# A four-layer decoder: state space decays as two 64x64 products, and new times in the planner's table

## The chip, the cores and the metric

One core of one Trainium2 chip runs the whole program. The metric is device time in microseconds (us) for one execution. A core has five engines that work side by side, each on its own queue of instructions in a fixed order: TensorE (PE in the profile: matrix products; PEld is its loading of weights), VectorE (DVE), ScalarE (ACT), GpSimd (POOL) and SyncE (SP, which issues transfers). An engine that reaches an instruction whose input isn't there waits, and everything queued behind it waits too.

## The reference

The input is 2048 tokens (32 sequences of 64) of 256 values. Twelve sublayers follow each other, each added to its input:

```python
x = x + _L0_attn_ref(_layernorm(x, axis=-1), ...)
x = x + _L0_xattn_ref(_layernorm(x, axis=-1), ctx_1024, ...)
x = x + _L0_ffn_ref(...)
x = x + _L1_attn_ref(...)    # state space model, 32 heads of 64, state 128
...
x = x + _L2_attn_ref(...)    # state space model, 8 heads of 64, state 128
...
x = x + _L3_ffn_ref(...)     # 64 experts, 6 of them for each token
return x
```

The change touches the two state space layers. Their core is a scan over the 64 steps of a sequence:

```python
dt = jax.nn.softplus(dt + dt_bias)
A = -jnp.exp(A_log)
dA = jnp.exp(dt * A)
def step(h, inp):
    dA_t, dt_t, x_t, B_t, C_t = inp
    u = (dt_t[:, :, None] * x_t)[..., None] * B_t[:, :, None, :]
    h = dA_t[:, :, None, None] * h + u
    y = jnp.einsum('bhpn,bhn->bhp', h, C_t)
    return (h, y)
```

A sequence is only 64 steps long, so the scan can be written as a 64x64 matrix for each head: entry (s, t) is C_t . B_s times the decay from s to t, which is the exponential of the sum of dt*A over the steps after s up to t.

## The kernel before

**Two layers of code.** The kernel doesn't call the engines in order. A Recorder (`net.nc`) takes each operation with its operands and finds what it depends on. When all of them are recorded, the class Order goes through them with a list schedule: it keeps a time for each engine (`free_at`), looks at the operations whose inputs will be there, and always takes the one that can start earliest, the recorded order breaking ties. Its result fixes the order of the instructions on all five engines, the buffers that tiles get, and the engine of each operation that may run on one of two (`either`: VectorE or ScalarE; `combine`: VectorE or GpSimd). The function issue then emits the program in this order; its line 2326 is therefore the line of every instruction in the profile.

**What the planner believes.** `duration` (line 456) gives each operation a time from its engine, its kind and the number of its elements; `latency` (line 488) is what passes between the end of an operation and the start of one on another engine that needs it. In `Order.run` an engine is free again at start + cost. An operation that needs one on its own engine alone may start, for the planner, when the first has started: the order of the queue keeps them apart. Nothing of this table is on the chip. It decides the order alone; the chip waits on semaphores, so an order planned with wrong times is still a correct one. Operations up to 120 us of TensorE work ahead of the oldest unfinished one may be planned (`Order(net.nc.ops, Net.SLOTS, 120.0)`).

**What is recorded.** Tokens are worked on in 16 tiles of 128 (two sequences each), in three groups of 8, 6 and 2 tiles. While a group goes through the last sublayers, the next goes through the first ones, and the recorder weaves the two. The state space layers work on two tiles (256 tokens) at a time and on eight heads at a time: `unit_ssm_heads` (line 1229) is called 4 times for each pair of tiles in the first of these layers and once in the second, so (4 + 1) x 8 = 40 times.

**The decays.** In `unit_ssm_heads`, `ra` is dt*A of the two tiles, eight heads and 64 columns, zero where the column comes before the row. The constant `after` (line 53) is a 128x128 matrix with a one where the row comes later than the column *and both are in the same sequence*: two 64x64 triangles on the diagonal, zeros elsewhere. `after` times `ra[:, t]` adds up the steps between. For each of the two tiles t that is one product with 128 rows, 128 columns of weights and 512 moving columns into one 512-wide PSUM tile `ps`; ScalarE then takes the exponential into `m`, VectorE multiplies with C.B. Later sixteen small 64x64 products of each tile use `m`; there, the halves b = 0 and b = 1 of the partitions write PSUM tiles of their own (`pv[b]`), as in the other places where 64-row products of the two halves occur (`cross_out`: a new `po` for each b).

Of the kernel before, what the change touches and what calls it, by code (L numbers as in the profile page):

```python
# [216 lines left out]
def split(ap, a, pat="p (a b) -> p a b"):  # L217
    return ap.rearrange(pat, a=a)
# [233 lines left out]
DMA = ("dma_start", "indirect_dma_start")  # L452
# [3 lines left out]
def duration(engine, method, args, kw):  # L456

    out = kw["out"] if "out" in kw else args[0]
    if method in DMA:
        return 0.06 if engine == "sync" else 1.3  # L460
    views = [v for v in [*args, *kw.values()] if isinstance(v, View)]
    n = max(v.size() for v in views)
    if engine == "tensor":
        lhsT, rhs = args[1], args[2]
        if method == "transpose":
            return 0.109
        k, m, n = lhsT.n, lhsT.size(), rhs.size()
        part = (32 if k <= 32 else 64 if k <= 64 else 128) * (32 if m <= 32 else 64 if m <= 64 else 128) / 16384

        if part == 1:  # L470
            return max(n, m) * 0.00168 + 0.004
        return max(0.068, n * 0.00168 * part * 1.2 + 0.02)
    small = any(v.size() == 1 and v.n > 1 for v in views) and n > 1
    if engine == "vector":
        return 0.15 + n * 0.00104 + 0.06 * small
    if engine == "scalar":
        return 0.115 + n * 0.00092 + 0.08 * small
    if method == "memset":
        return 0.2 + n * 0.0004
    if ALU.pow in args:  # L480
        return 0.4 + 0.157 * n
    if method == "tensor_copy":
        return 0.25 + n * 0.001
    full = sum(all(s for s, _ in v.dims) and v.size() == n for v in views[1:])
    return 0.14 + n * (0.00174 if full < 2 else 0.0022)


def latency(engine, op):

    return 0.25 if engine == "tensor" else 0.12  # L490


RESERVE = 4
# [2 lines left out]
class Order:  # L496
# [54 lines left out]
    def elsewhere(self, o, engine, since, end):  # L551


        for w, m in o.ways:
            if w != engine:
                other = max(self.free_at[w], since) + duration(w, m, o.args, o.kw)
                gain = {"vector": 1.0, "gpsimd": -1.0}[w] if {w, engine} == {"vector", "gpsimd"} else 0.0
                if other + gain < end:
                    return True
        return False  # L560

    def run(self):
        ready = {e: [] for e in self.ENGINES}

        def enter(op):
            for e, _ in op.ways:
                bisect.insort(ready[e], op, key=lambda o: o.at)

        for o in self.ops:
            if o.waits == 0:  # L570
                enter(o)
        done, oldest, result = [False] * len(self.ops), 0, []
        while len(result) < len(self.ops):
            limit = self.pos[oldest] + self.horizon
            best = None
            for e in self.ENGINES:
                now, seen = self.free_at[e], 0
                for o in ready[e]:
                    if self.pos[o.at] > limit or seen == 32:
                        break  # L580
                    seen += 1
                    since = o.ready
                    opens = [t for t in o.tiles if t.slot is None and t.tag in self.slots]
                    if opens:
                        if any(not self.free[t.tag] for t in opens):
                            continue
                        since = max([since] + [self.free[t.tag][0][0] for t in opens])
                    start = max(now, since)
                    method = next(m for w, m in o.ways if w == e)
                    cost = duration(e, method, o.args, o.kw)  # L590
                    key = start
                    if e == "scalar":
                        table = TABLES.get(getattr(o.args[2], "name", "") if method == "activation" else "", 0)
                        if table and table != self.table:
                            key += 1.3
                            cost += 1.3
                    if len(o.ways) > 1 and self.elsewhere(o, e, since, start + cost):
                        continue
                    if best is not None and (key, o.at) >= best[0] and not (
                        o is best[1] and start + cost < best[3] + best[4]  # L600
                    ):
                        continue
                    if opens and not self.may_open(o):
                        continue
                    best = ((key, o.at), o, e, start, cost, opens)
                    if key <= now:
                        break
            assert best is not None, "nothing can go on"
            _, o, e, start, cost, opens = best
            for w, _ in o.ways:  # L610
                ready[w].remove(o)
            for t in opens:
                t.slot = self.free[t.tag].pop(0)[1]
            end = start + cost
            self.free_at[e] = end
            if e == "scalar":
                m = next(m for w, m in o.ways if w == e)
                table = TABLES.get(getattr(o.args[2], "name", "") if m == "activation" else "", 0)
                self.table = table or self.table
            lat = latency(e, o)  # L620
            if o.ways[0][1] in DMA:
                v = next(v for v in o.outs + o.ins if isinstance(v, View) and v.dtype != I32)
                self.moved = max(self.moved, end) + v.n * v.size() * 4 / 300e3
                lat = 2.0 + self.moved - end
            for t in o.tiles:
                t.left -= 1
                if t.left == 0 and t.tag in self.slots:
                    bisect.insort(self.free[t.tag], (end + lat, t.slot))
            for n in o.after:
                same = len(n.ways) == 1 and n.ways[0][0] == e and o.ways[0][1] not in DMA  # L630
                n.ready = max(n.ready, start if same else end + lat)
                n.waits -= 1
                if n.waits == 0:
                    enter(n)
            done[o.at] = True
            while oldest < len(done) and done[oldest]:
                oldest += 1
            oldest = min(oldest, len(done) - 1)
            result.append((o, e))
        self.length = max(self.free_at.values())  # L640
        return result


class Net:
# [584 lines left out]
    def unit_ssm_heads(self, W, nh, g, j, st):  # L1229

        nc = self.nc
# [7 lines left out]
        ra = self.b4(2, 8, 64)  # L1239
# [5 lines left out]
            self.conv(par, cw, xs[:, u : u + 2, :], self.pair(wx, (j + u) * P, hT), j + u)  # L1245
        gs, m = self.b4(4, GT), self.b4(2, 8, 64)
        for t in range(2):
            ps = self.mm()
            self.prod(ps, [(self.k("after"), ra[:, t])])
            nc.scalar.activation(m[:, t], split(ps, 8), AF.Exp)  # L1250
        nc.vector.tensor_tensor(m, m, bc(cb, 2, 8), ALU.mult)
        for u in range(0, 4, 2):
# [2 lines left out]
        for t in range(2):  # L1255
            ps = split(self.mm(), 4)
# [11 lines left out]
        for t in range(2):  # L1268
            for u in range(4):
                for b in range(2):  # L1270
                    rb = slice(64 * b, 64 * b + 64)
                    for h in range(2):
# [4 lines left out]
                            start=True,  # L1277
                            stop=True,
# [17 lines left out]
        for u in range(4):  # L1296
# [4 lines left out]
            for t in range(2):  # L1301
# [4 lines left out]
                    start=(first and u == 0),  # L1306
                    stop=(last and u == 3),
# [830 lines left out]
    def experts(self, n):  # L2138
# [4 lines left out]
        for i in range(n):  # L2143
            self.unit_L3_parts(i)
            yield 0.2 / n

    def unit_L3_ffn(self, layer, W, g, run):
        nc = self.nc
        gate, su, sd = W
# [5 lines left out]
        for t in range(2):  # L2155
# [21 lines left out]
            nc.vector.reduce_sum(hot, one.rearrange("p k e -> p e k"), AX.X)  # L2177
            pn = self.mm()[:, :64]
            self.prod(pn, [(self.k("before"), hot)] + ([(self.k("ones"), run)] if i else []))
            if dense:  # L2180

                nc.vector.scalar_tensor_tensor(wn[:, t], sc, wr, hot, ALU.mult, ALU.mult)
                nc.vector.scalar_tensor_tensor(wn[:, t], pn, float(P), wn[:, t], ALU.is_lt, ALU.mult)
                nc.vector.tensor_tensor(run, run, hot, ALU.add)
                continue
# [239 lines left out]
```

## Time and profile before

| | |
|---|---|
| six runs before | median 3199.26 us (3193.6 to 3208.91) |
| the profiled execution | 3205.06 us, of which 3203.3 us between its first and last instruction |
| PE busy | 2993.4 us in 26862 products |
| DVE busy | 2216.9 us in 5239 instructions |
| ACT busy | 1414.0 us in 2623 |
| POOL busy | 1414.7 us in 1278 |
| products with `after` (128x512) | 79.6 us in 160 records |
| 64x64 products on 512 columns, in cross_out | 75.2 us in 512 records |

TensorE works on these 32-bit operands in two passes, so each recorded product is two records: 80 products with `after` are 160 records. Records of PE overlap, since a product's last results come out while the next one streams in; the time that a product really takes up is the distance from its start to the next start. VectorE's records overlap too: the lengths of all its records add up to 2434 us, while it is busy for 2216.9 us; ScalarE's add up to 1537 us against 1414.0 us.

### The profile page before, as it was taken

Reading aid. Unit: us, or ns where it says so; the run is one execution under the profiler, and the core shown is the slowest. Engines: PE = TensorE matmul, PEld = TensorE weight load, DVE = VectorE, ACT = ScalarE, POOL = GpSimd, SP = SyncE. Lnnn points to the kernel's source line nnn. Section 1 sums busy time; section 2 is a strip of 40 time slices with the busy share of each in tenths; the row PEclk is TensorE's granted clock in tenths of the full one; section 3 lists DMA queues with packets and bytes.
Section 4 is the critical chain, followed back from the end, with each engine's and each line's share of the span. In section 5 each row is a group of like instructions: output and inputs, shape, how many; then the busy total and the mean of one; then the engine's idle time right before and its main releaser. Section 6 shows DMA issues by size and latency. Waiting matters only on the chain.

```text
span 3203.3 us, 66434 instructions
## 1 busy us (share of the span) xinstructions
PE 2993.4 (93%) x26862; PEld 2382.5 (74%) x26862; DVE 2216.9 (69%) x5239; ACT 1414.0 (44%) x2623; POOL 1414.7 (44%) x1278
## 2 busy tenths in 40 slices
PE   8999999999999899999989999999999988986689
PEld 7888887777777788778767777767787767774467
DVE  5564347775457577665889987777667888776684
ACT  1233226565442233534545665553335745453341
POOL 4442233224454555225653356655534655354230
PEclk9999999999999899999999999999899999997689
DMA  4104120031421433011010010203561211224240
GB/s 153 33 23 171 54 96 1 3 141 57 200 107 47 156 110 117 31 64 61 27 47 10 8 58 8 79 17 127 180 217 62 88 43 41 76 85 128 80 176 27
DMA packets 112949, 256.97 MB, mean 80 GB/s; under 512 B 26309, under 2 KB 73688, under 8 KB 100228
## 3 DMA queue, kind: packets, MB, share of 16 engines
q1 hardware_dynamic: 97860, 204.73, 18.4%
q0 software_dynamic: 14784, 48.01, 4.4%
q8 instruction: 212, 3.47, 0.5%
q14 instruction: 93, 0.76, 0.1%
HBM read 177.34 MB, written 78.77 MB: 80 GB/s over the span
## 4 chain that ended last, share of the span: by engine, by line
PE 67%; DVE 20%; ACT 5%; POOL 5%; issue 3%; DMA 1%; SPq 0%; DVEq 0%; POOLq 0%; ACTq 0%
PE L_xattn_mm L2326 9%; PE cross_out_mm L2326 8%; PE L_attn_mm L2326 8%; PE ssm_heads_mm L2326 7%; PE pair_mm L2326 5%; DVE ssm_heads_b L2326 5%; PE L_ffn_mm L2326 4%; PE turn_mm L2326 4%; PE L_block_mm L2326 3%; PE rope_mm L2326 3%; DVE L_xattn_b L2326 2%; PE L_dense_mm L2326 2%; PE heads_mm L2326 2%; PE L_experts_mm L2326 2%; PE outrows_mm L2326 1%
## 5 line engine op out<-in xcount | busy, mean ns | idle before, releaser
L2326 PE MATMUL pair_mm<-norm_b,load_ssm_w 128*128 128x256 f32 x1280 | 306.4, 385 | 0.9 <-DVE ssm_heads_b L2326 0.6
L2326 PEld LDWEIGHTS pair_mm<-norm_b,load_ssm_w 128*128 128x128 f32 x1280 | 238.4, 192 | 44.4 <-issue 8.5
L2326 DVE SCALAR_TENSOR_TENSOR ssm_heads_b<-pair_mm,load_ssm_wp,ssm_heads_b 128x252 f32<-128x252 f32 (+2 forms) x480 | 218.7, 473 | 18.4 <-ACT ssm_heads_b L2326 8.5
L2326 POOL TENSOR_TENSOR L_xattn_sm<-L_xattn_sm,__init___consts 128x8 f32<-128x8 f32 (+2 forms) x62 | 178.5, 2882 | 88.2 <-DVE L_xattn_sm L2326 79.6
L2326 ACT ACT_TABLE_LOAD x153 | 196.3, 1283 | 33.8 <-PE L_block_mm L2326 11.7
L2326 POOL TENSOR_TENSOR norm_sm<-norm_sm,__init___consts 128x1 f32<-128x1 f32 (+1 forms) x142 | 88.8, 628 | 266.1 <-DVE norm_sm L2326 252.1
L2326 ACT COPY L_xattn_b<-L_xattn_mm 128x512 f32<-128x512 f32 x189 | 110.8, 588 | 189.0 <-PE L_xattn_mm L2326 188.8
L2326 ACT COPY turn_b<-turn_mm 128x512 f32<-128x512 f32 x202 | 113.1, 588 | 182.2 <-PE turn_mm L2326 178.9
L2326 PE MATMUL ssm_heads_mm<-load_ssm_w,ssm_heads_b 128*128 128x256 f32 x640 | 161.1, 396 | 6.7 <-issue 3.7
L2326 PE MATMUL rope_mm<-norm_b,load_L_attn_w 128*128 128x128 f32 x1280 | 160.8, 282 | 3.5 <-DMA load_L_attn_w<-in_a_wk 2.9
L2326 PEld LDWEIGHTS rope_mm<-norm_b,load_L_attn_w 128*128 128x128 f32 x1280 | 152.7, 196 | 8.7 <-issue 5.7
L2326 POOL TENSOR_TENSOR ssm_heads_b<-ssm_heads_b,ssm_heads_b 128x1024 f32<-128x1024 f32 x30 | 70.8, 2362 | 188.6 <-DVE ssm_heads_b L2326 142.4
L2326 PEld LDWEIGHTS ssm_heads_mm<-load_ssm_w,ssm_heads_b 128*128 128x128 f32 x640 | 119.4, 194 | 41.9 <-issue 19.8
L2326 PEld LDWEIGHTS L_xattn_mm<-norm_b,load_L_xattn_w 128*128 128x128 f32 x1024 | 119.4, 192 | 8.3 <-issue 7.0
L2326 PE MATMUL L_xattn_mm<-norm_b,units_L_xattn_w 128*128 128x128 f32 x1024 | 122.5, 277 | 2.1 <-ACT norm_b L2326 1.4
L2326 ACT ACTIVATE ssm_heads_b<-pair_mm,load_ssm_wp 128x256 f32<-128x256 f32 x160 | 81.6, 561 | 96.8 <-PE pair_mm L2326 94.9
L2326 POOL DMA_INDIRECT slots<-norm_b,L_ffn_sm x84 | 93.4, 1112 | 68.8 <-DVE L_ffn_b L2326 24.5
L2326 PE MATMUL L_xattn_mm<-norm_b,load_L_xattn_w 128*128 128x128 f32 x1024 | 123.1, 276 | 0.0
L2326 PEld LDWEIGHTS L_xattn_mm<-norm_b,units_L_xattn_w 128*128 128x128 f32 x1024 | 118.3, 192 | 4.3 <-ACT norm_b L2326 1.8
L2326 DVE TENSOR_TENSOR rope_b<-rope_mm,__init___consts 128x512 f32<-128x512 f32 x160 | 102.7, 679 | 25.1 <-PE rope_mm L2326 13.9
L2326 PE MATMUL cross_out_mm<-load_L_xattn_w,cross_out_b 128*128 128x256 f32 x512 | 118.1, 388 | 1.9 <-ACT cross_out_b L2326 1.9
L2326 PE MATMUL L_attn_mm<-load_L_attn_w,L_attn_b 128*128 128x256 f32 x512 | 119.3, 385 | 0.7 <-ACT L_attn_b L2326 0.5
(437 smaller groups left out, 7768.1 us busy)
## 6 DMA issues: line engine op xcount, KB each, us to landing
queue<-far_w SPq DMA_DIRECT2D x14, 1024.0 KB
L_block_w<-in_f_rows SPq DMA_DIRECT2D x16, 770.0 KB
load_ssm_w<-in_s_in SPq DMA_DIRECT2D x12, 1024.0 KB
parts<-far_w SPq DMA_DIRECT2D x10, 1024.0 KB
slots<-far_w SPq DMA_DIRECT2D x16, 548.0 KB
L_experts_b<-slots SPq DMA_DIRECT2D x32, 274.0 KB
units_L_xattn_w<-kept_x SPq DMA_DIRECT2D x8, 1024.0 KB
L_parts_b<-parts SPq DMA_DIRECT2D x14, 512.0 KB
```

The source lines that it names most:

```text
L2326: done = getattr(getattr(nc, e), method)(*map(real, op.args), **{k: real(v) for k, v in op.kw.items()})
```

## The change

There are two parts. The first replaces the product with `after` by two, one for each sequence, on 64 partitions and 64 columns of weights each; both write the same PSUM tile, on different partitions. The second rewrites the planner's `duration` for VectorE, ScalarE and GpSimd, shortens `latency`, lets an engine be free again a little before the operation's result is there (`EARLY`; `got` is the time of the result), and lets an operation that needs one on its own engine start 0.03 us after that one's result instead of at its start, except on TensorE and SyncE. The times of TensorE products are left as they are; for the planner, a 128x128 product on 512 columns takes 512 x 0.00168 + 0.004 = 0.864 us, and a 64x64 one 512 x 0.00168 x 0.25 x 1.2 + 0.02 = 0.278 us.

```diff
     if method in DMA:
-        return 0.06 if engine == "sync" else 1.3
+        return 0.06 if engine == "sync" else 1.28
...
     small = any(v.size() == 1 and v.n > 1 for v in views) and n > 1
+    psum = any(v.t.psum for v in views)
+    full = sum(all(s for s, _ in v.dims) and v.size() == n for v in views[1:])
     if engine == "vector":
+        if not psum and method in ("tensor_scalar", "tensor_copy", "tensor_scalar_add", "tensor_single_scalar"):
+            return 0.16 + n * 0.00052 + 0.11 * small
+        if method == "tensor_tensor" and not full and n > 64:
+            return 0.15 + n * 0.00205
+        if method.startswith("reduce") and views[1].dims[-1][0] > 1:
+            return 0.15 + n * 0.0017
         return 0.15 + n * 0.00104 + 0.06 * small
     if engine == "scalar":
-        return 0.115 + n * 0.00092 + 0.08 * small
+        if method == "activation":
+            return (0.17 if psum else 0.205) + n * 0.00083 + 0.18 * (small and psum)
+        return 0.16 + n * 0.00084 + 0.1 * small
     if method == "memset":
-        return 0.2 + n * 0.0004
+        return 0.2 + n * 0.00066
...
+EARLY = {"vector": 0.082, "scalar": 0.1, "gpsimd": 0.04}
+
 def latency(engine, op):
 
-    return 0.25 if engine == "tensor" else 0.12
+    return 0.2 if engine == "tensor" else 0.06
...
-            end = start + cost
+            got = start + cost
+            end = got if o.ways[0][1] in DMA else got - EARLY.get(e, 0.0)
             self.free_at[e] = end
...
-                    bisect.insort(self.free[t.tag], (end + lat, t.slot))
+                    bisect.insort(self.free[t.tag], (got + lat, t.slot))
             for n in o.after:
                 same = len(n.ways) == 1 and n.ways[0][0] == e and o.ways[0][1] not in DMA
-                n.ready = max(n.ready, start if same else end + lat)
+                n.ready = max(n.ready, (start if e in ("tensor", "sync") else got + 0.03) if same else got + lat)
...
         for t in range(2):
+
             ps = self.mm()
-            self.prod(ps, [(self.k("after"), ra[:, t])])
+            for b in range(2):
+                rb = slice(64 * b, 64 * b + 64)
+                nc.tensor.matmul(ps[rb], self.k("after")[rb, rb], ra[rb, t], start=True, stop=True)
             nc.scalar.activation(m[:, t], split(ps, 8), AF.Exp)
```

More of the change, by code (lines that the diff above doesn't have):

```diff
@@ L483, in duration @@
         return 0.25 + n * 0.001
-    full = sum(all(s for s, _ in v.dims) and v.size() == n for v in views[1:])
     return 0.14 + n * (0.00174 if full < 2 else 0.0022)
+EARLY = {"vector": 0.082, "scalar": 0.1, "gpsimd": 0.04}
 def latency(engine, op):
-    return 0.25 if engine == "tensor" else 0.12
+    return 0.2 if engine == "tensor" else 0.06
 RESERVE = 4
@@ L622, in run @@
                 v = next(v for v in o.outs + o.ins if isinstance(v, View) and v.dtype != I32)
-                self.moved = max(self.moved, end) + v.n * v.size() * 4 / 300e3
-                lat = 2.0 + self.moved - end
+                self.moved = max(self.moved, got) + v.n * v.size() * 4 / 300e3
+                lat = 2.0 + self.moved - got
             for t in o.tiles:
```

## The prediction

> **What bounds the kernel now.** I read the page first: busy times, then the slices.
>
> ```profile
> span 3203.3 us, 66434 instructions
> PE 2993.4 (93%) x26862; PEld 2382.5 (74%) x26862; DVE 2216.9 (69%) x5239; ACT 1414.0 (44%) x2623; POOL 1414.7 (44%) x1278
> ...
> PE   8999999999999899999989999999999988986689
> ...
> PEclk9999999999999899999999999999899999997689
> ...
> PE 67%; DVE 20%; ACT 5%; POOL 5%; issue 3%; DMA 1%; SPq 0%; DVEq 0%; POOLq 0%; ACTq 0%
> ```
>
> TensorE sets the time: 93% busy, and 67% of the chain that ended last. It is idle for 3203.3 - 2993.4 = 210 us, and that is all that a better order can win directly. The busy times by stretch of 200 us show where this lies (the columns after the length: PE, PEld, DVE, ACT, POOL, granted clock, share of the DMA engines, GB/s).
>
> ```profile
> 400.00:600.00 200.00, 198.53 (x1465) 162.55 (x1464) 133.91 (x311) 93.84 (x151) 65.27 (x55) 1.00 0.12 39
> 1600.00:1800.00 200.00, 181.22 (x1718) 139.93 (x1716) 175.07 (x393) 109.34 (x195) 92.72 (x76) 0.97 0.07 23
> 2600.00:2800.00 200.00, 179.81 (x1844) 140.02 (x1842) 170.82 (x393) 91.81 (x197) 101.25 (x96) 0.97 0.15 49
> 2900.00:3000.00 100.00, 63.65 (x622) 44.59 (x621) 65.66 (x266) 31.54 (x67) 39.94 (x40) 0.74 0.44 135
> 3000.00:3100.00 100.00, 73.63 (x744) 51.42 (x745) 72.34 (x206) 42.56 (x85) 36.72 (x36) 0.74 0.20 72
> ```
>
> Up to 1000 us TensorE is nearly gapless. From 2900 to 3100, near the end, it idles 63 of 200 us and runs at a granted clock of 0.74; the whole end from 2800 on holds 78 us of idle time. The remaining 210 - 78 = 132 us are spread over the stretches before, the two largest pieces (19 and 20 us) where VectorE is busy for over 170 of 200 us. What TensorE waits for, by the view of waits:
>
> ```profile
> PE norm_mm L2326 <- DVE norm_b L2326: 26.3, 12, 7.9
> PE small_scores_mm L2326 <- ACT keys_apart_b L2326: 17.0, 13, 2.8
> PE turn_mm L2326 <- POOL L_xattn_b L2326: 15.1, 8, 5.4
> ```
>
> Three engines and many short waits: a matter of order, not of one late producer.
>
> **Part one, the two blocks.** The 80 products become 160, the PE records 160 become 320, with 160 more loads of weights; no DMA, no work on another engine, no new wait but that the exponential needs both halves. What does the array's time do? I read the timeline of PE (start, us, then the group):
>
> ```profile
> 581.36 1.88 PE L2326 MATMUL ssm_heads_mm<-ssm_heads_b,__init___consts 128*128 128x512 f32 x4
> 583.08 0.59 PE L2326 MATMUL pair_mm<-norm_b,load_ssm_w 128*128 128x256 f32 x2
> ...
> 278.62 1.95 PE L2326 MATMUL cross_out_mm<-turn_b,context_cx 64*64 64x512 f32 x16
> ...
> 1277.69 0.60 PE L2326 MATMUL ssm_heads_mm<-__init___consts,ssm_heads_b 128*128 128x128 f32 x4
> 1278.22 0.64 PE L2326 MATMUL L_attn_mm<-turn_b,L_attn_b 64*64 64x256 f32 x2
> 1278.79 0.44 PE L2326 MATMUL ssm_heads_mm<-__init___consts,ssm_heads_b 128*128 128x128 f32 x2
> ```
>
> Two full products (4 records) take 583.08 - 581.36 = 1.72 us, 0.43 a pass. The sixteen records of cross_out are eight 64x64 products: they start four at a time, one on each quarter of the array, every 0.43 us, and 4 x 0.43 = 1.72 us is the whole group without its end. So a quarter streams 512 columns no faster than the whole array; only using all four quarters gains. The change uses two of the four, those on the diagonal: 2 x 0.43 = 0.86 us a tile, as before. Streaming: 80 x (0.86 - 0.86) = **0**. The planner, which books 2 x 0.278 = 0.556 us, believes it saves 25 us; the rows show none of it.
>
> What is added is the change of shape. Before 1278.22, four records of 128 columns should stream 4 x 0.107 = 0.43 us, but 0.53 pass: 0.10 lost on the way in. The two records of 256 columns should take 0.43 us, but 0.57 pass: 0.14 lost. The first pass of 128x128 after such a change takes about 0.11 us longer, because its weights can't be loaded ahead. About 0.35 us for a visit. I counted the neighbours of the products with `after` in the order of PE's records: they stand in 45 groups, 32 of them between 128x128 products on both sides, 13 with a smaller shape on one side (there the change of shape only moves). 32 x 0.35 = **+11 us**, on the engine that sets the time, nothing covering it. A plan that places the visits beside other 64-row work brings it to 0; one that splits every pair makes it 80 x 0.35 = 28.
>
> No row shows one thing: two products of different partition halves writing one PSUM tile at once. Everywhere in this kernel the halves have tiles of their own. Bounds: side by side, 0.86 us a tile; one after the other, 4 passes of 0.43 = 1.72. I take the first, since neither rows of the array nor output partitions are shared; the second is a rival. The Trainium skill, TensorEngine Tiling (Array Packing), section "Gotcha 1: PSUM Pressure", speaks against the change here: different row tiles cannot access the same PSUM bank at the same time. By that rule the sum would get the 80 x 0.86 us of that rival; no run here shows it. The same page's "Theoretical Speedup" gives up to 2x for a dimension of 64, which would be a gain; the row of cross_out shows that it comes only with the other quarters filled.
>
> **Part two, the table.** It costs the chip nothing; it moves instructions. First, is it nearer to the rows?
>
> ```profile
> L2326 ACT ACTIVATE ssm_heads_b<-pair_mm,load_ssm_wp 128x256 f32<-128x256 f32 x160 | 81.6, 561 | 96.8 <-PE pair_mm L2326 94.9 <-PE L_xattn_mm L2326 1.0 <-DVE ssm_heads_b L2326 0.6
> L2326 DVE TENSOR_TENSOR ssm_heads_b<-ssm_pre,__init___consts 128x1024 f32<-128x1024 f32 x7 | 14.3, 2041 | 0.0
> L2326 POOL MEMSET values_b<- 128x576 f32 x32 | 18.6, 580 | 10.1 <-PE pair_mm L2326 7.3 <-PE small_scores_mm L2326 1.4 <-DVE L_attn_b L2326 0.8
> ```
>
> The first: 0.431 us by the old formula, 0.563 by the new, 0.561 in the trace. The second: 1.21, 2.25, 2.04. The third: 0.43, 0.58, 0.58. The application of the norm on VectorE (192 of them): 0.476 and 0.403, with a median of 0.410 and a mean of 0.535. `EARLY` follows the overlap of records: VectorE's lengths sum to 2434 us against 2217 busy, so the old table booked this engine 217 us too full, ScalarE 1537 - 1414 = 123. So the old planner took VectorE for 9% slower than it is, just where (1600 to 1800, 175 of 200 us) it is nearly full, sent work to GpSimd instead, and let products come late in TensorE's queue.
>
> What that is worth, no row prices. Upper bound of the gain: all the spread idle time, 132 us, and none is reached by a plan that still has to wait for DMA and chains; lower: a loss, worked out as a rival. The long end is a chain of dependent steps (TensorE idle there at 63 and 74 busy of 100), which an order shortens little. I take a quarter of the spread time, **-33 us**, since the errors corrected are 5 to 10% of the other engines' times and the waits are short.
>
> Sum: 3205.1 + 0 + 11 - 33 = 3183, a change of -22. The profiled execution is 5.8 us above the median of the six runs; on the median, 3199.3 - 22 = 3177. I predict **3177 us**; with the gain between 15 and 70 and the visits between 0 and 28, some 3130 to 3195.
>
> **The rivals.**
>
> *The halves write one after the other.* For it: every other place keeps them apart. Against: different output partitions. 80 x 0.86 = 69 us on TensorE: 3177 + 69 = 3246. It decides as soon as more than 22/0.86, about 26, of the 80 pairs are serialized.
>
> *The plan is too tight.* The old one had slack by mistake; the new one has none, and where VectorE and GpSimd slow each other the new times are too short: the norms' mean of 0.535 against 0.403 is 192 x 0.13 = 25 us, and the 55 subtractions and scalings of 1024 elements on VectorE at 1.3 to 1.9 us in place of 1.215 another 20. Each is a wait in a fixed queue, mostly in 1600 to 2000 and 2600 to 2800. If these 45 us come back at TensorE and the gain of 33 falls away: 3199 + 11 + 45 = 3255 at most, about half of it likely, 3232. Slower from the point where less than 11 us of idle time go.
>
> *It cancels.* The plan wins about what the visits cost: 3199 + 11 - 11 = 3199. For it: the waits are short and TensorE is 93% full anyway.
>
> **Chances.** Forecast 0.55, cancels 0.15, too tight 0.18, one after the other 0.12. About 0.3%, 10 us, is what a measurement tells from no change: below 3190 faster, above 3209 slower. A tenth of the forecast's share falls inside; a few hundredths of the cancelling case fall on either side: faster 0.54, same 0.16, slower 0.30. The range leaves out the far ends: 3120 to 3246.
>
> **What would show it.** The 320 records of 64x64 on `after`: pairs that start within 0.01 us and a next pass 0.43 us later (right), or starts 0.43 us apart for the halves (the first rival). PE busy up by about 11 us or less, idle time before 2800 us down from 132 to about 100, the GpSimd count of 1024-element operations down. Wrong would be a stretch of 200 us with more than 30 us of new idle time, or a longer end after 2800: I have assumed that the end stays.

## The result and the profile after

The changed kernel takes a median of 3221.55 us over 30 runs (3205.05 to 3265.55), the kernel before 3205.66 us over 67 runs beside it: a ratio of **1.0052, 95% interval 1.0040 to 1.0064**. It is slower by half a per cent, where 0.7% faster was forecast. The profiled execution after has a span of 3218.6 us. Its page:

```profile
span 3218.6 us, 66679 instructions
PE 3000.6 (93%) x27022; PEld 2360.8 (73%) x27022; DVE 2119.3 (66%) x5260; ACT 1418.3 (44%) x2637; POOL 1360.9 (42%) x1233
...
PE   8999999999999999999989999999999999986689
...
PEclk9999999999999999999989999999999999997689
...
PE 66%; DVE 20%; ACT 5%; POOL 4%; issue 3%; DMA 2%; SPq 0%; DVEq 0%; POOLq 0%; ACTq 0%
```

TensorE has 7 us more to do. It is idle for 3218.6 - 3000.6 = 218 us against 210. VectorE is busy for 98 us less, although the lengths of its records add up to 2434.8 us (2434.0 before): the same work, packed closer. GpSimd has 54 us less. So the new table did move and pack the work of the other engines, and the engine that sets the time got nothing of it. The stretches that the prediction read, after:

```profile
400.00:600.00 200.00, 195.95 (x1346) 154.15 (x1347) 117.84 (x289) 88.46 (x145) 68.44 (x57) 1.00 0.10 35
1600.00:1800.00 200.00, 180.95 (x1763) 136.43 (x1764) 168.69 (x414) 107.02 (x191) 93.78 (x77) 0.96 0.07 22
2600.00:2800.00 200.00, 185.85 (x1847) 141.64 (x1846) 163.80 (x391) 96.00 (x197) 103.09 (x95) 0.94 0.15 50
2900.00:3000.00 100.00, 63.73 (x598) 44.39 (x592) 58.81 (x259) 33.70 (x68) 40.31 (x41) 0.75 0.44 135
3000.00:3100.00 100.00, 73.43 (x814) 50.95 (x814) 61.29 (x199) 41.61 (x88) 36.05 (x36) 0.76 0.27 89
```

In every one of them VectorE (the third pair of numbers) is less busy than before, by 6 to 16 us. TensorE's idle time is the same at 1600 (19 us) and from 2900 to 3100 (63 us), where VectorE was thought to hold it up; only 2600 to 2800 gained, 6 us. Over the whole stretch up to 2800 us the idle time is 133.0 us before and 132.8 after, 2800 less the first number of PE:

```profile
0.00:2800.00 2800.00, 2667.04 (x24104) 0.98 0.22 77
2800.00:3400.00 600.00, 326.37 (x2760) 0.89 0.20 68
```

before, and after:

```profile
0.00:2800.00 2800.00, 2667.18 (x24231) 0.98 0.22 77
2800.00:3400.00 600.00, 333.42 (x2793) 0.90 0.21 69
```

That zero is made of gains and losses. PE alone, before:

```profile
0.00:200.00 200.00, 186.40 (x1860) 1.00 0.21 75
1000.00:1200.00 200.00, 182.09 (x1502) 0.94 0.36 114
2000.00:2200.00 200.00, 189.71 (x1769) 0.97 0.20 69
2600.00:2800.00 200.00, 179.81 (x1844) 0.97 0.15 49
```

and after:

```profile
0.00:200.00 200.00, 183.22 (x1934) 1.00 0.21 75
1000.00:1200.00 200.00, 190.10 (x1683) 0.97 0.37 120
2000.00:2200.00 200.00, 186.59 (x1757) 0.94 0.18 63
2600.00:2800.00 200.00, 185.85 (x1847) 0.94 0.15 50
```

200 minus the first number of PE is its idle time. 1000 to 1200 wins 8.0 us and 2600 to 2800 6.0; the first 200 lose 3.2 and 2000 to 2200 3.1. Summed over the fourteen stretches, 19.3 us are won in five and 19.2 lost in nine. The waits tell the same:

```profile
PE norm_mm L2343 <- DVE norm_b L2343: 27.2, 8, 8.3
PE turn_mm L2343 <- DVE L_xattn_b L2343: 17.6, 7, 5.8
PE small_scores_mm L2343 <- ACT keys_apart_b L2343: 13.3, 11, 2.6
```

The first was 26.3 us and is 27.2. The transposes now wait for VectorE, 17.6 us (4.5 before), where the longest wait of theirs was 15.1 us for GpSimd (10.9 after): the wait has moved, not gone.

### The profile page after: what moved, and what is told of

It is laid out like the page before. It is cut to its first block, busy times and chain, and to the rows that moved or that the text cites. A ratio compares the mean times of both kernels' runs of the same rounds, so it can differ in the third digit from the quotient of the medians.

```text
span 3218.6 us, 66679 instructions
## 1 busy us (share of the span) xinstructions
PE 3000.6 (93%) x27022; PEld 2360.8 (73%) x27022; DVE 2119.3 (66%) x5260; ACT 1418.3 (44%) x2637; POOL 1360.9 (42%) x1233
## 4 chain that ended last, share of the span: by engine, by line
PE 66%; DVE 20%; ACT 5%; POOL 4%; issue 3%; DMA 2%; SPq 0%; DVEq 0%; POOLq 0%; ACTq 0%
PE ssm_heads_mm L2343 9%; PE cross_out_mm L2343 8%; PE pair_mm L2343 8%; PE L_xattn_mm L2343 8%; PE L_attn_mm L2343 7%; PE L_ffn_mm L2343 4%; PE turn_mm L2343 3%; PE rope_mm L2343 3%; PE L_block_mm L2343 2%; DVE L_xattn_b L2343 2%; DVE ssm_heads_b L2343 2%; DVE L_attn_b L2343 2%; PE L_dense_mm L2343 2%; PE L_experts_mm L2343 2%; DVE L_xattn_sm L2343 1%
## 5 line engine op out<-in xcount | busy, mean ns | idle before, releaser
L2343 ACT COPY turn_b<-turn_mm 128x512 f32<-128x512 f32 x237 | 130.9, 589 | 172.0 <-PE turn_mm L2343 169.9
L2343 DVE SCALAR_TENSOR_TENSOR ssm_heads_b<-pair_mm,load_ssm_wp,ssm_heads_b 128x252 f32<-128x252 f32 (+2 forms) x480 | 193.4, 466 | 12.0 <-ACT ssm_heads_b L2343 11.6
L2343 PE MATMUL rope_mm<-norm_b,load_L_attn_w 128*128 128x128 f32 x1280 | 167.8, 287 | 5.4 <-DMA load_L_attn_w<-in_a_wk 5.2
L2343 DVE TENSOR_TENSOR __init___x<-__init___x,cross_out_mm 128x256 f32<-128x256 f32 x32 | 13.5, 420 | 186.8 <-PE cross_out_mm L2343 186.7
L2343 POOL TENSOR_TENSOR L_attn_b<-rope_b 128x256 f32<-128x256 f32 x131 | 98.1, 765 | 75.7 <-DVE rope_b L2343 55.8
L2343 POOL TENSOR_TENSOR ssm_heads_b<-ssm_heads_b,ssm_heads_b 128x1024 f32<-128x1024 f32 x26 | 63.4, 2437 | 155.7 <-DVE ssm_heads_b L2343 144.6
L2343 POOL TENSOR_TENSOR heads_b<-heads_b,heads_sm 128x1024 f32<-128x1024 f32 x46 | 87.7, 1908 | 88.6 <-DVE heads_sm L2343 70.2
L2343 DVE TENSOR_SCALAR norm_b<-__init___x,norm_sm,norm_sm 128x256 f32<-128x256 f32 x192 | 95.5, 514 | 43.8 <-POOL norm_sm L2343 37.0
```

The costliest lines, as they stand in the source:

```text
L2343: done = getattr(getattr(nc, e), method)(*map(real, op.args), **{k: real(v) for k, v in op.kw.items()})
```

## The experiments

Each ratio compares a kernel with the kernel before on the same chip. Five sets of runs went to five chips. On those of the first, fourth and fifth set the kernel before takes 3324 to 3326 us, on those of the second and third 3194 to 3200; why that matters is told under the fourth set. Each chip was used for one set only, so no run separates the chip from the occasion. All kernels compute the whole result.

**First set: the parts.** The blocks without a new order: before's plan, in which one operation is issued as two.

```diff
+            if getattr(op, "name", None) == "halves":
+                for b in range(2):
+                    rb = slice(64 * b, 64 * b + 64)
+                    ps, w, v = op.args
+                    nc.tensor.matmul(real(ps[rb]), real(w[rb, rb]), real(v[rb]), start=True, stop=True)
+                continue
```

> The program of before in exactly its order on every engine; only each product with `after` is issued as two 64x64 ones. Theory V (visits: the blocks stream no faster and each visit among 128x128 products costs 0.35 us): 32 visits x 0.35 = 11 us more than before, 0.2 to 0.5% slower, PE busy up by 5 to 11 us. Theory O (the new order alone costs the time): no difference to before, within 0.1%. Theory S (the blocks save, as the planner's 0.278 us believes): 25 us less.

1.0013 (0.9995 to 1.0031). The table without the blocks:

```diff
-            for b in range(2):
-                rb = slice(64 * b, 64 * b + 64)
-                nc.tensor.matmul(ps[rb], self.k("after")[rb, rb], ra[rb, t], start=True, stop=True)
+            self.prod(ps, [(self.k("after"), ra[:, t])])
```

> The new table plans the program with the whole 128x128 products. Theory V: with the visits gone, about 11 us less than after, so 3 to 6 us above before (0.1 to 0.2%). Theory O: as slow as after, 0.5% above before. My prediction's step (the table wins 33 us) would give 1% less than before; I no longer expect it, because the idle time before 2800 us is 133 us in both traces.

1.0006 (0.9990 to 1.0021). The changed kernel's order without its blocks (planned with two blocks, issued as one product in the place of the second):

```diff
+                kind, ps, w, v = op.name
+                if kind == "whole":
+                    nc.tensor.matmul(real(ps), real(w), real(v), start=True, stop=True)
+                continue
```

> The program of after in exactly its order on every engine; each pair of 64x64 products is issued as one 128x128 product at the place of the second. Theory V: after's 36 visits between whole products are gone, 12 us less than after, 0.1 to 0.2% above before. Theory O: no difference to after, 0.5% above before.

1.0030 (1.0014 to 1.0045). And the blocks planned with the old table, which is the first part of the change alone:

```diff
-            self.prod(ps, [(self.k("after"), ra[:, t])])
+            for b in range(2):
+                rb = slice(64 * b, 64 * b + 64)
+                nc.tensor.matmul(ps[rb], self.k("after")[rb, rb], ra[rb, t], start=True, stop=True)
```

> The first part of the change alone: two 64x64 products recorded and planned by the old table, which books 0.278 us for each. Theory V: 11 us plus or minus what another order is worth, so 0 to 0.7% above before. Theory O: as before, within what another order is worth.

1.0035 (1.0019 to 1.0051). No part gains, and none reaches the half per cent, though the intervals of the last two come near it. The changed kernel itself wasn't run on this chip, so its 1.0052 can't be added up from these four.

**Second set: is it the planner's wrong price of the blocks?** The changed kernel once more, and the same with the one price that the rows contradict put right (a 64x64 block passes 512 columns twice in 0.43 us each, two blocks side by side, so 0.43 for each; the table says 0.278):

```diff
+        if k == m == 64 and n == 512 and lhsT.t.tag == "consts":
+            return 0.432
```

> After once more, on the chip of this group of runs, to stand beside the three below: 0.3 to 0.6% above before.

1.0059 (1.0027 to 1.0091).

> After, but the planner books 0.432 us for each 64x64 product with `after`, so 0.864 a pair, which is what a pair takes up in the trace (two passes of 0.43 us), in place of 0.556. Theory P (0.2% of the loss comes from a plan that takes 80 pairs for 0.31 us cheaper than they are, as e4 against e1 and e3 against e2 suggest): 0.2% less than after again, 0.1 to 0.3% above before. Rival R (e4 and e3 are just other orders, and any other order moves the time by 0.2 to 0.3%): anywhere within 0.3% of after.

1.0122 (1.0096 to 1.0148). A truer time made the plan worse, by 0.6%, which is outside both expectations. So I asked what a change with no meaning does: the kernel before, with the planner's horizon at 117 instead of 120.

```diff
-    order = Order(net.nc.ops, Net.SLOTS, 120.0)
+    order = Order(net.nc.ops, Net.SLOTS, 117.0)
```

> Before, with the planner's horizon at 117 us in place of 120: another order that knows neither more nor less. It measures what a change of order alone is worth. Rival R: 0.2 to 0.4% away from before on either side. Theory P: within 0.1%.

1.0118 (1.0092 to 1.0145): more than twice the effect of the change under study, and three times the most that either expectation allowed. Its page:

```profile
span 3231.6 us, 66426 instructions
...
PE 3025.9 (94%) x26862; PEld 2403.5 (74%) x26862; DVE 2204.8 (68%) x5225; ACT 1424.0 (44%) x2632; POOL 1423.0 (44%) x1285
```

Idle time is 3231.6 - 3025.9 = 205.7 us, less than the 210 of before. The same products were busy for 32 us longer: the mean granted clock is 0.954 against 0.964 (0.951 to 0.954 in its five runs, 0.959 to 0.969 in the twelve of before beside it). An order sets not only how long TensorE waits but what clock it is given. The fourth kernel took aim at the changes of shape of the matmuls (TensorE's records show 1190 of them before, by my count of neighbours with another number of rows or columns): the new table, with 0.17 us booked for each change, and the shape in use preferred where it costs at most 0.1 us.

```diff
+                    if e == "tensor" and shape_of(o) != self.shape:
+                        key += 0.1
+                        cost += 0.17
```

> The new table with whole products, and one thing that neither table has: a TensorE product whose shape (32, 64 or 128 rows and columns) differs from that of the one before is booked 0.17 us longer and ranked 0.1 us later. The order then changes shape 461 times, in place of 1149. Theory W (the largest cost missing in the table is the change of shape: in the trace 0.10 us to the first pass after it and 0.05 to 0.11 within that pass): 690 x 0.17 = 117 us less, less what is lost where a product that others wait for stands back; 1.5 to 3.5% below before. Rival: TensorE's order becomes worse for the other engines by as much, and nothing is won.

1.0373 (1.0343 to 1.0402). The changes fell to 521, and the time rose.

```profile
span 3329.4 us, 66523 instructions
...
PE 3050.3 (92%) x26862; PEld 2508.9 (75%) x26862; DVE 2158.2 (65%) x5336; ACT 1375.9 (41%) x2566; POOL 1347.3 (40%) x1220
```

Its clock is 0.924. Here are the spans of all profiled executions on chips of this kind, divided up (idle = span - PE busy; clock = what the mean clock leaves out, (1 - clock) x span; the rest is PE busy - that):

| kernel | span | idle | of it before 2800 | lost to the clock | rest |
|---|---|---|---|---|---|
| before | 3203.3 | 210 | 133 | 115 (0.964) | 2878 |
| after | 3218.6 | 218 | 133 | 119 (0.963) | 2882 |
| after, again | 3204.1 | 210 | 127 | 112 (0.965) | 2882 |
| blocks at 0.432 | 3237.5 | 216 | 132 | 130 (0.960) | 2892 |
| old table, 117 | 3231.6 | 206 | 131 | 149 (0.954) | 2877 |
| old table, 123 | 3232.4 | 215 | 132 | 145 (0.955) | 2872 |
| new table, whole, 117 | 3217.4 | 222 | 147 | 106 (0.967) | 2890 |
| new table, whole, 123 | 3246.1 | 227 | 153 | 127 (0.961) | 2893 |
| table and shapes | 3329.4 | 279 | 194 | 253 (0.924) | 2797 |
| shapes and clock | 3385.4 | 322 | 221 | 244 (0.928) | 2819 |

Between before and the table with shapes the rest falls by 81 us for 669 changes of shape, 0.12 us each on the average. It is paid for with 69 us of idle time and 138 us of clock. This division is rough, because the fifth column also counts half clock while TensorE idles. Counted as half of its busy time at half clock, the loss is 94 us before and 224 with table and shapes; then the gain is 73 us (0.11 us a change) and the clock's part 130.

**Third set: draws or tables.** Old and new table, each at two more horizons. First the kernel before at 123:

```diff
-    order = Order(net.nc.ops, Net.SLOTS, 120.0)
+    order = Order(net.nc.ops, Net.SLOTS, 123.0)
```

> The kernel before with the planner's horizon at 123 instead of 120: the old table, whole products, another order. Theory A (a re-plan is a draw: any other order of this work moves the time by up to a per cent or so, and the order before lies near the favourable end): ratio to the kernel before between 1.000 and 1.015. Rival B (the old table's orders all lie near 1.000, and the 1.012 of horizon 117 is one unlucky case): ratio 0.997 to 1.003.

1.0108 (1.0075 to 1.0141). The new table with whole products, with the same line at 117.0 and at 123.0:

> The new table with the whole products (as in the run of the table alone), with horizon 117 instead of 120. Theory A (a draw of the same spread under either table): ratio to the kernel before 0.998 to 1.015, on either side of the 1.0118 that the old table gave at this horizon. Rival C (the new table plans better orders than the old one on the average, and only the order before is a lucky one): ratio below 1.005, so that old minus new at horizon 117 is at least 0.7%. Rival D (the new table plans worse orders): above 1.013.

1.0101 (1.0075 to 1.0128), beside 1.0118 for the old table at 117 on another chip.

> The new table with the whole products, horizon 123. Theory A: ratio to the kernel before 0.998 to 1.015, and its difference from the old table's run at 123 has no fixed sign. Rival C: at least 0.5% below the old table's run at 123. Rival D: at least 0.5% above it.

1.0126 (1.0100 to 1.0152), beside 1.0108. Theory A holds, C and D don't: the two pairs differ by -0.17% and +0.18%. The table above has the direct answer to the forecast: with the new table TensorE's idle time before 2800 us is 127 to 153 us, with the old one 131 to 133. The equal times of the two pairs hide a difference that has one direction: the new table's orders idle 16 us more at 117 and 21 more at 123, and have the higher clock (0.963 to 0.967 in its runs against 0.951 to 0.954, and 0.961 to 0.965 against 0.955 to 0.959). What these two plans lose in waits they about get back in clock; why their clock is higher, no run shows.

The last of this set adds to table and shapes a rule that puts small products off when the area put through TensorE of late is below half (`lack` in us, `work` the time weighted by the share of the array in use):

```diff
+                        low = max(0.0, self.lack + 0.5 * max(0.0, start - now)) > 0.6
+                        if low and work < 0.5 * cost:
+                            key += 2.0
```

> The new table with whole products, where the planner also books 0.17 us for each change of the matmul's shape, favours the shape in use a little (as in the run of table and shapes), and in addition puts off small products when the area that it has put through TensorE in the last microseconds is less than half of full, so that small products don't stand in a row for long. About half of before's changes of shape are planned. Theory E (the loss of the run of table and shapes was the granted clock, 505 us at half clock against 233, and its idle gaps): time at half clock 230 to 330 us, changes of shape 550 to 650, ratio to before 0.98 to 1.01. Rival F (small products in a row are not what halves the clock): half clock stays at 450 us or more, ratio 1.03 and above. If the putting off only turns into idle time of TensorE, the clock is up and the idle time is over 300 us.

1.0586 (1.0555 to 1.0616); clock 0.928 (488 us at half clock), idle 322 us, 621 changes. The numbers are those of rival F, but they don't decide, since the plan never kept the area up on the chip: by the count that the last section explains, 138 of its steps of 3.41 us stay below an area of 1500, against 148 with table and shapes and 77 before. Those of them without idle time (TensorE busy for over 99%) fell from 58 to 35; the others rose, so the putting off became idle time. As a remedy it failed. On rival F itself the count in the last section decides.

**Fourth and fifth set: the parts again, and the pair at 119.** The first three kernels are those of the first set; in the others the same line has 119.0, with the old table and, last, with the new one and whole products.

> The order before on every engine, each decay product issued as two 64x64 blocks in its place (as in blocks in the old order, whose chip had the kernel before at 3326 us). Theory (a visit of the blocks costs 0.35 us, some 32 to 36 visits, nothing else): ratio to the kernel before 1.002 to 1.004 where all of it counts, 1.000 to 1.002 where part of it falls into waits. If the blocks were the main cause of the changed kernel's 1.0052, it would be 1.005 here.

1.0010 (0.9995 to 1.0024).

> The new table with whole products (as in the run of the table alone). If the table is worth nothing at equal horizon, the ratio is 0.998 to 1.003 on this chip too. If the first run was near 1.000 only because that chip's waits on transfers hid a worse order, 1.005 to 1.013, as the other orders gave.

0.9996 (0.9981 to 1.0011).

> The changed kernel's own order with each pair of blocks issued as one whole product. If the order is what costs 0.5%: 1.004 to 1.006 and the blocks nothing. If order and blocks share it as on the first chip: 1.002 to 1.004. If the blocks are all of it: 0.999 to 1.001.

1.0022 (1.0008 to 1.0037).

> The kernel before with horizon 119. If orders are draws with no memory of the setting next to them: anything from 1.000 to 1.013, most likely near the mean of the orders so far, 1.007. If the time is a smooth function of the horizon with its least value at 120: 1.001 to 1.004, a third of the 1.0118 at 117.

0.9932 (0.9917 to 0.9947): the first order that is faster than before, by another meaningless step.

> The kernel before with horizon 119 once more. Its 0.9932 came on the chip where the kernel before takes 3324 us. If the order is better whatever the chip, the ratio is 0.990 to 0.997 again; if its gain belonged to that chip's waits alone, 0.998 to 1.013 on a chip where the kernel before takes 3200 us.

0.9924 (0.9902 to 0.9945). It repeats on a second chip.

> The new table with whole products, horizon 119: the fourth pair of orders at equal horizon. If the table is worth nothing and each order is a draw: anything from 0.99 to 1.013, with no tie to the old table's 0.9932. If the horizon of 119 is what makes the order good: within 0.3% of the old table's run at 119 beside it. If the new table plans better when the horizon suits: below 0.990.

1.0022 (1.0001 to 1.0043). At horizon 119 the new table's order is 1.0% slower than the old table's, on the same chip. Again it idles more (177 us before 2800 us against 152) at a higher clock (0.951 against 0.943, medians of the runs), but here the clock doesn't make up for it. So the horizon isn't what makes an order good either.

Both of these sets met chips of the slower kind again. What differs there? The kernel with the blocks in the old order, on it:

```profile
span 3329.6 us, 66758 instructions
...
PE 3053.8 (92%) x27022; PEld 2399.5 (72%) x27022; DVE 2215.6 (67%) x5239; ACT 1413.9 (42%) x2623; POOL 1411.2 (42%) x1278
...
PE 69%; DVE 16%; ACT 4%; issue 4%; POOL 3%; another core or an unknown queue 2%; DMA 1%; SPq 0%; POOLq 0%; DVEq 0%; ACTq 0%
```

VectorE, ScalarE and GpSimd take as long as before. TensorE is idle for 276 us against 210, the clock is 0.944, and 2% of the chain wait on something that the profile doesn't name. There the five orders other than before's have ratios from 0.992 to 1.004, on the faster chips six have 1.005 to 1.013. How an order stands to another doesn't carry over safely, and **the order of horizon 119 is known to be faster than before only on the slower chips**; it wasn't tried on the faster ones, nor beside the changed kernel.

## Why the prediction was wrong

**The step that failed** is the price of the table: "I take a quarter of the spread time, -33 us". It is the one term that no row priced, and it carried the forecast. Measured: idle time before 2800 us went from 133.0 to 132.8 us. At equal horizon the new table against the old one gave -0.17%, +0.18%, 0.0% (two runs) and +1.0%: no gain in any of four pairs that exceeds its uncertainty. In three of these pairs the idle time that the term was to reduce rose, by 16, 21 and 25 us.

*The premise under it* was misread: "so the old table booked this engine 217 us too full" takes the 217 us by which VectorE's records overlap for an error of the planner. The planner's own books say otherwise (`end - start` of each operation in `Order.run`, added up by engine, from the two kernels as they stand). With the old table VectorE is booked for 2265 us and was busy for 2217: 2% too full, not 9%. With the new table it is booked for 1849 us and was busy for 2119: 13% too empty. ScalarE goes from 1453 booked and 1414 busy to 1290 and 1418. The costs of VectorE's single operations add up to nearly the same in both plans (2265 and 2277); they were already near the busy time, and `EARLY` then takes off another 0.082 us for each of 5228 operations, 429 us in all. So the new table fits some rows better and the engines as a whole worse. That this is why the plans with it idle more fits the three pairs, but no run isolates it: the table without `EARLY` wasn't tried.

*What it got right.* A plan that takes VectorE for faster sends less work to GpSimd. The products of two 1024-element tiles there, before and after:

```profile
L2326 POOL TENSOR_TENSOR ssm_heads_b<-ssm_heads_b,ssm_heads_b x30: 2348/2362/2382, 507.4 to 2558.9; 128x1024 f32<-128x1024 f32 x30
```

```profile
L2343 POOL TENSOR_TENSOR ssm_heads_b<-ssm_heads_b,ssm_heads_b x26: 2351/2360/3552, 511.6 to 2555.6; 128x1024 f32<-128x1024 f32 x26
```

Four fewer, as foretold. *Where the inference broke* is "and let products come late in TensorE's queue". That VectorE is busy for 175 of 200 us where TensorE idles 19 didn't show that VectorE's load causes the 19: after, it is busy for 169 and TensorE idles 19 again. In the eight executions of the table whose plan doesn't keep to a shape, the idle time before 2800 us stays between 127 and 153 us. That it is set by the chains between sublayers is likely from the waits on norm_b (26.3 and 27.2 us), but no run isolated it.

*What the step left out* is the spread. I costed a re-plan by its intention and gave a loss only through a named mechanism. Any edit of the planner draws another order, and the orders of this kernel lie about 1% apart: 1.0118 and 1.0108 for two meaningless settings on the faster chips, 0.993 for a third on the slower ones, against a wanted gain of 1%. On chips like that of the forecast all six other orders that don't keep to a shape are slower than before's, so a draw was more likely to lose than to win. The draws do have one sign beforehand, the length that the planner itself gives its plan (`self.length`). For the old table at 119, 120, 117 and 123 it is 2983, 2989, 2997 and 3006 us, and the ratios are 0.993 (slower chips), 1, 1.0118 and 1.0108. For the new one with whole products at 120, 119, 117 and 123 it is 2909, 2922, 2927 and 2939 us, and the ratios are 1.000, 1.002 (slower chips), 1.010 and 1.013. Within one table a shorter plan was a faster one, but for one pair that its uncertainty doesn't tell apart; between the tables the length says nothing (2909 against 2989 us at about the same time). The blocks planned with the old table (2976 us, 1.0035) don't fit in, as the planner books their products 25 us too short. These are few orders, on chips of two kinds. Why before's order is a good one on the faster chips, no run shows beyond that; the view of the clock below explains where the loss of horizon 117 went, not why it was drawn.

**The blocks, streaming (0 us): right.** The timeline of PE after (start, us, then the group):

```profile
502.76 1.89 PE L2343 MATMUL pair_mm<-norm_b,load_ssm_w 128*128 128x256 f32 x8
504.59 1.93 PE L2343 MATMUL ssm_heads_mm<-ssm_heads_b,__init___consts 64*64 64x512 f32 x8
506.45 1.35 PE L2343 MATMUL pair_mm<-norm_b,load_ssm_w 128*128 128x256 f32 x5
```

Eight records are four blocks, two tiles. They take 506.45 - 504.59 = 1.86 us, four passes of 0.43 and 0.14 more. Single records start at 504.587 and 504.594, then 505.067 and 505.074: the halves run side by side, 7 ns apart.

**One after the other (3246 us): refuted** by these starts. Taken two by two in their order, 146 of the 160 pairs of these records start 6 or 7 ns apart. The rule that the Trainium skill gives in TensorEngine Tiling (Array Packing), section "Gotcha 1: PSUM Pressure", that different row tiles can't use one PSUM bank at the same time, doesn't hold for this pair: two blocks on the diagonal, with other rows, other columns and other partitions of the tile, write one tile in the time of one.

**The visits (+11 us): the cost of one visit right, the sum not pinned down.** In the group above, the eight records of 256 columns before it start 0.216 us apart, so they should stream 8 x 0.216 = 1.73 us; they take 1.82, so 0.09 is lost on the way in, 0.14 inside, and 0.10 in the first pass after: about 0.33, near the 0.35 foretold. PE's records show 78 changes of shape more than before. In before's own order the blocks cost 0.10 and 0.13% on the slower chips, 3 to 4 us, with intervals from -2 to 8 and to 10: less than the 11, so a part of it probably falls into waits, but neither run is clear of zero. The changed kernel's 1.0052 and 1.0059 against 1.0022 and 1.0030 for its order with whole products suggest 10 us, but across chips of two kinds, so this difference is an estimate. With some 3 to 10 us for the visits and 7 to 10 for the order (0.22 and 0.30% of 3325) the 16 that were measured can be made up; the exact division on the faster chips stays open, since the parts weren't run there.

**The end from 2800 us: "I have assumed that the end stays."** It holds 85 us of idle time in the profiled execution and 83 in the repeat, against 77. A longer end was named as what would make the forecast wrong; it did so by 6 to 8 us.

**The rivals.** Taken from the median before, the time went up by 16 us: halfway between the case that cancels (0) and the plan that is too tight (3232 - 3199 = 33). The condition of the latter, less than 11 us of idle time won, came true. The plan is too tight by the books above, and by more than the 45 us that the rival priced. That this cost the 16 us isn't shown: no stretch got 10 us of new idle time, and correcting the one underbooked time that was tried made the kernel slower. Its weight of 0.18 was too small because the bare spread of orders, which gives the same time without any mechanism, had no weight at all.

## What to carry to other kernels

Before pricing an edit to a planner, find out how far the time moves when nothing meaningful is changed (one constant, three values, same chip). If that spread is as large as the gain that is hoped for, a forecast of the mean is "no change" with the spread as its range, and a measured gain of one plan may be a drawn order and not a better table. Compare the parts, idle time and clock, over several such settings too: here they showed a steady effect of the table that the total time hid. Idle time of the bounding engine next to a busy engine isn't idle time caused by it: look for the same idle time in another order before counting it as winnable. And before calling a planner's table too full, add up what it books for an engine and compare that with the engine's busy time, not with the lengths of its records.

## What the runs showed of the hardware

**Small products halve the clock without any idle time.** From the kernel of table and shapes, the timeline, then busy time of PE, granted clock, DMA:

```profile
171.85 29.75 PE L2353 MATMUL L_attn_mm<-L_attn_b,L_attn_b 32*128 32x64 f32 x480
```

```profile
168.00:173.00 5.00, 5.00 (x34) 1.00 0.00 0
173.00:176.30 3.30, 3.30 (x65) 1.00 0.12 19
176.30:193.00 16.70, 16.70 (x320) 0.50 0.45 135
193.00:210.40 17.40, 16.59 (x139) 0.50 0.00 1
```

480 records on 32 of the 128 rows (in part several at once, on different rows) follow each other from 171.85 to 201.6 us. TensorE is never idle up to 193 us, and yet 4.4 us after they begin, one whole step of the clock's 3.41 us, it drops from 1.00 to 0.50 and stays there. In 3.30 us at full clock 65 of them pass, 64 columns of a quarter of the array each: 65 x 64 x 0.25 = 1040 full-height columns, where a full array, at 0.43 us for 512 columns (0.84 ns each), passes about 3300/0.84 = 3900. The Trainium skill, in TensorE: Matmul & The Clock Gate, section "What's actually happening", tells of a window of 3413 ns and of half clock after an idle one. The steps agree; the condition, by these lines, isn't idleness but how much of the array is in use.

I counted it over all steps of 3.41 us of the eight executions in the table above whose plan doesn't keep to a shape (7504 steps), as columns times the shares of rows and columns in use, each record in the step in which it starts; a full step has about 4070. Below 1500 the next step ran at half clock in 0.80 of the cases from full clock and in 0.91 from half; between 1500 and 2000 in 0.02 and 0.21; above 2000 in one of 6336 steps. Idle time alone doesn't decide it: of 30 steps at full clock with less than 1500 in which TensorE was busy for over 99%, 19 were followed by half clock; of 13 with more than 2000 in which it idled for over 40%, none.

Between before and the table with shapes the steps below 1500 rose from 77 to 148, those of them without idle time from 16 to 58. So the 138 us have two causes: small products in a row, and more idle time. By this count an order that mixes large products among small ones should keep the clock up, and one that groups small products, which saves about 0.12 us a change, should lose it. An order that has both advantages wasn't found.

**Two kinds of chip.** Identical orders give 3200 us on one and 3325 on the other, and up to 800 us from the start the two run alike (TensorE busy for 778.6 of 800 us before, 779.1 for its order with the blocks on a slower chip); from there on the slower one waits more and is granted less (730.5 against 749.2 us busy from 1600 to 2400, clock 0.94 against 0.96). What causes it, and whether it is the chip or the occasion, no run shows.
